# Keys of a multi-head attention: laid out by TensorE with a 0/1 matrix, or by a trip through DRAM

## Chip, cores, metric

The kernel runs on one core of a Trainium2 chip. The metric is device time in microseconds (us) of one execution, given as the median of several. Beside it there is one profiled execution, whose trace gives every instruction's start and duration.

## What is computed

Four layers work on x, 2048 tokens by 128 features, in float32. In the order of the reference:

```python
x = x + 0.5 * L0_ffn(norm(x)); x = x + L0_attn(norm(x)); x = x + 0.5 * L0_ffn(norm(x))
x = x + 0.5 * L1_ffn(norm(x)); x = x + L1_attn(norm(x)); x = x + 0.5 * L1_ffn(norm(x))
x = x + 0.5 * L2_ffn(norm(x)); x = x + L2_attn(norm(x)); x = x + 0.5 * L2_ffn(norm(x))
x = x + 0.5 * L3_ffn(norm(x)); x = x + L3_attn(norm(x)); x = x + 0.5 * L3_ffn(norm(x))
```

L0 is a low-rank product and a causal attention of one head, L1 a mixture of eight experts and a convolution. The parts that matter here come after them. L2_ffn is a gated two-layer product (silu(gate) * up, then down). L2_attn and L3_attn have 16 heads of 8 features with rotary position encoding; L3_attn is causal. L3_ffn is called twice: it holds a 16-head attention of its own whose scores are scaled per query by a sigmoid, a norm, and eight experts of which each token takes one:

```python
scores = einsum('bhqd,bhkd->bhqk', q, k) / sqrt(hd)
scores = scores * (sigmoid(einsum('bhsd,hd->bhs', q, scale_w)) * 2)[..., None]
out = softmax(scores) @ v
x = ln(src + (out * sigmoid(out @ gate_w + gate_b)) @ out_w)
x = ln(x + selected_expert(x) * weight)
```

So four big attentions over 2048 tokens and 16 heads run one after the other: L2's (rope2), that of the first L3_ffn (gated0), L3's own (rope3, causal), and that of the second L3_ffn (gated1).

## The kernel before

The tokens are cut into four chunks c of 512. For each of the four attentions `attend` (L856) walks through steps. A unit is a query chunk and a group g of four heads, so there are 16 units. In every step it may issue three things on TensorE. `score` makes a 128x1024 piece of q·k into the tile `sn`, and VectorE reduces its maximum. `weight` makes the transposed piece k·q into `st`, with the maxima already subtracted by extra rows, and ScalarE takes the exponential into `pr`. `accumulate` multiplies by the values into `av`. A unit's weights can start only when its scores are complete and its maxima have been turned and written back into the query tile.

There are three modes. "fill" runs from an attention's first step until its first weight; "core" is the steady state; "drain" begins when all its scores are issued and the first scores of the next attention take their place. Outside is "free". Norms and projections for the next layer run as side tasks (`beside`): at every step the first two in the list each issue one more part. Their order on each engine is otherwise fixed when the kernel is built.

A head has 8 features. Queries and keys are split into a rounded part (hi) and the rest (lo), so that a product of 64 rows holds hi, lo and two cross terms, and two rows of ones carry the maxima. The key tile `kp` has 128 rows (two heads of 64 rows), 8 head pairs and 2048 tokens. Its rows for one head are khi, klo, khi, klo (32 rows), two rows of ones and 30 of zeros. The projection gives hi and lo in another order: features of all heads along the 128 rows. `send("k", c)` (L688) therefore writes hi and lo to DRAM (`dk`, two DMAs of 256 KB), and `load_keys` (L707) reads them back into place with eight DMAs of 128 KB per chunk, issued by SP (SyncE). Queries go the same way through `dq`, and `begin` (L865) reads those of one unit back with two DMAs. SP issues its DMAs in order. `head_buffers` (L1408) fills the rows of ones and zeros of `kp` by eight DMAs of 512 KB from a small table `rest`.

The norm is `norm` (L177): statistics on VectorE, `inv_sqrt` (L161) with a shift, a subtraction and three Newton steps of three VectorE operations on 128x4 elements. Outside the drain ScalarE then applies scale and shift (`on_act`), for which one more VectorE operation makes `nb`. `ring` (L583) hands out most temporary 128x512 tiles from ten buffers; `wide_tile` hands out the buffers of `pr`. `put` (L600) copies a small product out of PSUM. `Experts.run` gathers tokens and weights with indirect DMAs on Pool (GpSimd), multiplies, writes to DRAM, gathers back with 16 indirect DMAs (`yg`, L1350), and `tail` norms each chunk.

Of the kernel before, what the change touches and what calls it, by code (L numbers as in the profile page):

```python
# [11 lines left out]
F32 = mybir.dt.float32  # L12
F32R = mybir.dt.float32r
I32 = mybir.dt.int32
# [17 lines left out]
NG = 4  # L32
NEG = -1.0e30
# [9 lines left out]
def tile_macaron(ctx: ExitStack, tc: tile.TileContext, a: dict, out: bass.AP):  # L43
# [8 lines left out]
    turn = {"load": 0, "evac": 0, "q": 0, "qp": 0}  # L52
# [15 lines left out]
    order = {"pinned": False, "mode": "free"}  # L68
# [25 lines left out]


    ident = const.tile([P, P], F32, name="ident")
    make_identity(nc, ident)
    anti = const.tile([P, P], F32, name="anti")
# [32 lines left out]
    iota_pi = const.tile([P, P], I32, name="iota_pi")  # L131
# [17 lines left out]
    for n in ("shift", "aT", "bT", "cT"):  # L149
        kr_in.append(const.tile(list(a[n].shape), F32, name=n))  # L150
        loads[len(kr_in) % 2].dma_start(out=kr_in[-1], in_=a[n])
# [9 lines left out]
    def inv_sqrt(pool, var, shape, tag):  # L161
        v = pool.tile(shape, F32, tag=tag + "_v", name=tag + "_v")
        vec.tensor_scalar_add(v, var, 1e-5)
        g = pool.tile(shape, I32, tag=tag + "_g", name=tag + "_g")
        vec.tensor_single_scalar(g, v.bitcast(I32), 1, op=ALU.logical_shift_right)
        vec.tensor_scalar(g, g, -1.0, float(0x5F3759DF), ALU.mult, ALU.add)
        r = pool.tile(shape, F32, tag=tag + "_r", name=tag + "_r")
        prev = g.bitcast(F32)
        for _ in range(3):
            h = pool.tile(shape, F32, tag=tag + "_h", name=tag + "_h")  # L170
            vec.tensor_tensor(h, prev, prev, ALU.mult)
            vec.scalar_tensor_tensor(h, h, -0.5, v, ALU.mult, ALU.mult)
            vec.scalar_tensor_tensor(r, h, 1.5, prev, ALU.add, ALU.mult)
            prev = r
        return r

    def norm(src, dst, on_act=False):  # L177
        stats = small.tile([P, TC, 6], F32, tag="ln_stats", name="ln_stats")
        mv = small.tile([P, TC, 2], F32, tag="ln_mv", name="ln_mv")
        for t in range(TC):  # L180
            vec.bn_stats(stats[:, t, :], src[:, t, :])
            vec.bn_aggr(mv[:, t, :], stats[:, t, :])
        rstd = inv_sqrt(small, mv[:, :, 1], [P, TC], "ln")
        if on_act:
            nb = small.tile([P, TC], F32, tag="ln_nb", name="ln_nb")
            vec.scalar_tensor_tensor(nb, mv[:, :, 0], -1.0, rstd, ALU.mult, ALU.mult)
        for t in range(TC):
            if on_act:
                nc.scalar.activation(  # L189
                    dst[:, t, :], src[:, t, :], AF.Identity, bias=nb[:, t : t + 1], scale=rstd[:, t : t + 1]  # L190
                )
            else:
                vec.tensor_scalar(
                    dst[:, t, :], src[:, t, :], mv[:, t, 0:1], rstd[:, t : t + 1], ALU.subtract, ALU.mult
                )
# [387 lines left out]
    def ring(name, tag="w", shape=(P, CW), bufs=10):  # L583
        return pools["ring"].tile(list(shape), F32, tag=tag, name=name, bufs=bufs)
# [15 lines left out]
    def put(dst, src):  # L600
        if order["mode"] == "drain":
            vec.tensor_copy(dst, src)
        elif order["mode"] == "fill":
            nc.scalar.copy(dst, src)
        else:
            evac(dst, src)
# [61 lines left out]
    class Heads:  # L668
# [3 lines left out]
        def __init__(self):  # L672
            self.current = False
            self.queries = {}
            self.units = [(qc, g) for qc in range(NC) for g in range(NG)]
            self.scores, self.weights = [], []
            for u in self.units:
                nk = u[0] + 1 if self.causal else NC
                nkb = (u[0] + 1) * TC if self.causal else NT
                if u == self.units[0]:  # L680
                    self.scores += [(self, u, t, kc) for kc in range(nk) for t in range(TC)]
                else:
                    self.scores += [(self, u, t, kc) for t in range(TC) for kc in range(nk)]
                self.weights += [(u, kb) for kb in range(nkb)]
            self.scored = 0
            self.waiting_keys, self.loaded, self.sent, self.valued, self.ready = [], set(), set(), set(), set()

        def send(self, which, c):  # L688
            hi, lo = ring("hi"), ring("lo")
            yield from self.project(which, c, hi.bitcast(F32R), lo.bitcast(F32R))  # L690
            parts = (hi, lo, lo, hi) if which == "q" else (hi, lo)
            d = (dq if which == "q" else dk)[c]
            for n, part in enumerate(parts):
                queue().dma_start(out=d[:, n * HD : (n + 1) * HD, :], in_=part)
            if which == "q":
                self.sent.add(c)
            elif self.current:
                self.load_keys(c)
            elif order["mode"] == "drain":
                self.load_keys(c, (0,))  # L700
                self.waiting_keys.append((c, (1,)))
            else:
                self.waiting_keys.append((c, (0, 1)))
            yield 1


        def load_keys(self, c, halves=(0, 1)):  # L707
            for h in halves:
                ps = slice(4 * h, 4 * h + 4)
                for j in range(2):  # L710
                    for n in range(2):
                        r = j * KD + n * 2 * HD
                        nc.sync.dma_start(
                            out=kp[r : r + 2 * HD, ps, c * CW : (c + 1) * CW].bitcast(F32),
                            in_=rows_of(dk[c], j)[:, ps, :],
                        )
            if 0 in halves:
                self.loaded.add(c)

        def prepare(self, c):  # L720
            yield from self.normed(c)
            self.ready.add(c)
            yield from self.send("k", c)
            if c == 0:
                yield from self.send("q", 0)
# [14 lines left out]
        def query(self, c):  # L740
            yield from self.send("q", c)
# [114 lines left out]
    def attend(A, carried, follow, after=None):  # L856
# [3 lines left out]
        A.current = True  # L860
        for c, halves in A.waiting_keys:
            A.load_keys(c, halves)
# [139 lines left out]
        beside = [[0, task] for task in (*carried, own)]  # L1002
# [3 lines left out]
        while nw < len(weights) or last:  # L1006
# [12 lines left out]
            if s and s[3] not in B.loaded:  # L1019
                s = None  # L1020
# [28 lines left out]
            for entry in beside[:2]:  # L1049
                if entry[0] <= n:  # L1050
                    later = next(entry[1], None)
                    if later is None:
                        beside.remove(entry)
                    else:
                        entry[0] = n + later
# [11 lines left out]
        A.current = False  # L1067
# [24 lines left out]
    class Experts:  # L1092
# [82 lines left out]
        def run(self, carried, after):  # L1175
# [76 lines left out]
            def turned(b):  # L1252
# [7 lines left out]
                for k in range(n):  # L1260
                    s = s0 + k
                    xt = ring("xt", "xt", (P, D), 4)
# [134 lines left out]
    dk = [dram.tile([NH, 2 * HD, CW], F32, name=f"dk{c}") for c in range(NC)]  # L1397
    dq = [dram.tile([NH, 4 * HD + 2, CW], F32, name=f"dq{c}") for c in range(NC)]
    def zero_tables():
        with tc.tile_pool(name="zero2", bufs=1) as tmp:  # L1400
            zero = tmp.tile([KD, 2, CW], F32, name="zero2")
            nc.vector.memset(zero, 0.0)
            for c in range(NC):
                nc.sync.dma_start(out=dq[c][:, 4 * HD :, :], in_=zero[0:NH, :, :])
            nc.vector.memset(zero[0:2, 0, :], 1.0)
            nc.sync.dma_start(out=rest, in_=zero[:, 0, :])

    def head_buffers(pool):  # L1408
# [4 lines left out]
        for j in range(2):  # L1413
            r = slice(j * KD + 4 * HD, (j + 1) * KD)
            for c in range(NC):
                nc.sync.dma_start(
                    out=kp[r, :, c * CW : (c + 1) * CW].bitcast(F32),
                    in_=rest[0:n, :].unsqueeze(1).to_broadcast([n, NH // 2, CW]),
                )
            for qp in qps:  # L1420
                nc.sync.dma_start(
                    out=qp[r, :, :].bitcast(F32), in_=rest[2 : n + 2, :].unsqueeze(1).to_broadcast([n, 2, CW])
                )
        nc.gpsimd.memset(va_flat, 1.0)
        return kp, va_flat, qps

    w3p = ctx.enter_context(tc.tile_pool(name="w3p", bufs=1))
    w2p = ctx.enter_context(tc.tile_pool(name="w2p", bufs=1))
    with tc.tile_pool(name="w1p", bufs=1) as w1p:
# [17 lines left out]
    kp, va_flat, qps = head_buffers(heads)  # L1447
# [5 lines left out]
    pools["av"] = ctx.enter_context(tc.tile_pool(name="av_ps", bufs=1, space=PSUM))  # L1453

# [8 lines left out]
    experts = [Experts(w3, g) for g in gated]  # L1463
    for c in range(NC - 1):
        finish_all([l2_chunk(c, w2), rope2.prepare(c)])
    carried = [chain([l2_chunk(NC - 1, w2), rope2.prepare(NC - 1)])]
# [23 lines left out]
def _layout(i):  # L1490
# [44 lines left out]

    sw = np.zeros((NH, HD, NH, HD), f)
# [36 lines left out]
```

## Time and profile before

| | |
|---|---|
| median of 3 runs | 4061.76 us (4051.71 to 4081.86) |
| profiled execution | 4074.4 us |
| its span | 4072.6 us |
| its mean granted TensorE clock | 0.885 |
| TensorE busy | 3557.4 us (87%) |
| VectorE busy | 3141.5 us (77%) |
| ScalarE busy | 2329.1 us (57%) |
| Pool busy | 215.0 us (5%), 262 instructions |

The page puts busy times per engine first, then the span in 40 slices, the DMA queues, the chain that ended last, the costliest groups of instructions and the DMA issues. A line of the groups reads: line in the code, engine, operation, output <- inputs, shapes, count | busy time, mean of one in ns | idle time of the engine just before, and what ended it. PE is TensorE, PEld its weight loads, DVE VectorE, ACT ScalarE, POOL GpSimd, SPq the issues of SyncE's queue. A row of a stage table has the window, then busy time and count per engine, the granted clock (1.00 is full), the DMA engines' busy share and GB/s.

The trace gives the stages:

| stage | us |
|---|---|
| L0 and L1 | 0 to 664 |
| L2_ffn and rope2's keys, first scores, first weights at 851 | 664 to 851 |
| rope2 core; drain | 851 to 1466; to 1565 |
| fill of gated0, first weights at 1663 | 1565 to 1663 |
| gated0 core and drain | 1663 to 2345 |
| experts 0, rope3's keys, first score 2573.5, first weights 2594.8 | 2345 to 2595 |
| rope3 core; drain | 2595 to 3077; to 3166 |
| fill of gated1, first weights at 3211 | 3166 to 3211 |
| gated1 core and drain | 3211 to 3896 |
| experts 1, tail, store | 3896 to 4072.6 |

### The profile page before, as it was taken

To read this page: it belongs to the slowest core of one execution; us is meant where nothing else is said; L and a number is where in the kernel's file an instruction comes from. 1 tells how busy PE (TensorE), PEld (TensorE's weight loads), DVE (VectorE), ACT (ScalarE), POOL (GpSimd) and SP (SyncE) were. 2 spreads that over 40 slices of the span, in tenths; PEclk is the share of its full clock that TensorE was granted. 3 is DMA by queue.
4 is the path that set the end of the run, shared out by engine and by line. 5 is a ranking of instruction groups with operands and counts; after the bars stand their busy time and mean duration, and the time that the engine had idled before them with its cause. 6 is when DMAs were issued, how large, how long until landed. Compare 5 with 4: busy or idle time off the path is not lost. (4 is left out here: it accounts for less than half of the span.)

```text
span 4072.6 us, 72035 instructions
## 1 busy us (share of the span) xinstructions
PE 3557.4 (87%) x29080; PEld 1680.4 (41%) x29080; DVE 3141.5 (77%) x5645; ACT 2329.1 (57%) x4436; POOL 215.0 (5%) x262
## 2 busy tenths in 40 slices
PE   8789898689999995899999965599997899999965
PEld 8566664333333342333333343243333333333334
DVE  3855443579999975899999745689997799999844
ACT  1222122158888862688888722246675488888732
POOL 2000000100000000000000033100000000000013
PEclk8889798779999997899999966668998799999966
DMA  2100003220000002100000022400002200000012
GB/s 71 25 1 1 1 1 87 62 63 7 10 7 10 4 13 57 50 9 9 7 10 4 9 70 77 110 20 10 10 2 62 54 10 7 10 7 7 7 42 74
DMA packets 71532, 111.91 MB, mean 27 GB/s; under 512 B 9712, under 2 KB 29920, under 8 KB 70944
## 3 DMA queue, kind: packets, MB, share of 16 engines
q1 hardware_dynamic: 57536, 77.81, 7.2%
q0 software_dynamic: 7088, 20.81, 2.1%
q10 hardware_dynamic: 6576, 8.69, 0.8%
q8 instruction: 229, 3.75, 0.4%
q14 instruction: 103, 0.84, 0.1%
HBM read 74.47 MB, written 31.75 MB: 26 GB/s over the span
## 5 line engine op out<-in xcount | busy, mean ns | idle before, releaser
L83 DVE TENSOR_REDUCE h_mx<-sn 128x2 f32<-128x1024 f32 (+1 forms) x1856 | 2206.3, 1197 | 141.4 <-PE sn L886 119.8
L942 ACT ACTIVATE pr<-st 128x512 f32<-128x512 f32 x3712 | 1972.7, 585 | 518.7 <-PE st L75 335.7
L75 PE MATMUL av<-pr,va 128*32 128x256 f32 x14592 | 1191.4, 399 | 10.9 <-ACT h_ot L971 10.9
L75 PE MATMUL st<-qp,kp 64*128 64x512 f32 x3712 | 998.4, 500 | 49.2 <-ACT pr L942 45.6
L886 PE MATMUL sn<-kp,qp 64*128 64x512 f32 (+3 forms) x3712 | 812.1, 416 | 126.6 <-DMA qp<-dq 46.1
L75 PEld LDWEIGHTS st<-qp,kp 64*128 64x128 f32 x3712 | 394.4, 188 | 818.1 <-ACT pr L942 441.8
L75 PEld LDWEIGHTS av<-pr,va 128*32 128x32 f32 x14592 | 293.1, 109 | 664.7 <-issue 626.8
L886 PEld LDWEIGHTS sn<-kp,qp 64*128 64x128 f32 x3712 | 388.7, 195 | 186.6 <-issue 99.8
L75 PE MATMUL h<-xnT,w_l_w12T 128*128 128x512 f32 x512 | 250.1, 611 | 1.7 <-DVE xnT L65 1.7
L554 ACT ACTIVATE hid<-h 128x512 f32<-128x512 f32 x128 | 76.4, 597 | 301.4 <-PE h L75 301.4
L75 PEld LDWEIGHTS po<-w_l_w3T,hid 128*128 128x128 f32 x1024 | 131.2, 193 | 69.1 <-DVE hid L555 47.2
L563 DVE SCALAR_TENSOR_TENSOR x<-po,gate,x 128x128 f32<-128x128 f32 x256 | 71.9, 344 | 100.4 <-PE po L75 100.3
L75 PE MATMUL po<-w_l_w3T,hid 128*128 128x128 f32 x1024 | 139.9, 279 | 1.3 <-DVE hid L555 1.3
L555 DVE TENSOR_TENSOR hid<-hid,h 128x512 f32<-128x512 f32 x128 | 87.2, 683 | 55.1 <-PE h L75 55.1
L75 PEld LDWEIGHTS h<-xnT,w_l_w12T 128*128 128x128 f32 x512 | 90.2, 197 | 66.1 <-issue 62.6
L1270 POOL DMA_INDIRECT wt<-in_b_wt,w_row_i x30 | 28.8, 960 | 1436.6 <-DVE slot_i L83 1395.0
L915 ACT CAST h_mT<-mt_ps 8x512 fp32r<-8x512 f32 x64 | 36.9, 576 | 100.4 <-PE mt_ps L93 100.2
L83 DVE BATCH_NORM_STATS2 st<-ph 128x6 f32<-128x256 f32 x46 | 19.9, 432 | 87.0 <-PE ph L75 87.0
L223 POOL TENSOR_TENSOR x<-x,w_b_n2b 128x512 f32<-128x512 f32 x8 | 10.1, 1266 | 1301.1 <-DVE rows L83 1133.7
L93 PE MATMUL xn_tp<-ident,xn_t 128*128 128x128 f32 x64 | 20.1, 406 | 66.3 <-ACT xn_t L189 62.7
L83 DVE TENSOR_TENSOR sn<-sn,mask_qk 128x256 f32<-128x256 f32 x128 | 54.2, 426 | 30.7 <-PE sn L886 29.3
L83 DVE TENSOR_TENSOR st<-st,mask_kq 128x128 f32<-128x128 f32 x256 | 63.3, 291 | 14.0 <-PE st L75 13.4
(391 smaller groups left out, 2627.5 us busy)
## 6 DMA issues: line engine op xcount, KB each, us to landing
qp<-dq SPq DMA_DIRECT2D x128, 136.0 KB
kp<-dk SPq DMA_DIRECT2D x128, 128.0 KB
dq<-hi SPq DMA_DIRECT2D x23, 256.0 KB
dq<-lo SPq DMA_DIRECT2D x23, 256.0 KB
wt<-in_b_wt SPq DMA_DIRECT2D x16, 258.0 KB
kp<-rest SPq DMA_DIRECT2D x8, 512.0 KB
dk<-lo SPq DMA_DIRECT2D x16, 256.0 KB
qp<-h_mT SPq DMA_DIRECT2D x256, 4.0 KB
```

The costliest lines, as they stand in the source:

```text
L75: pin(nc.tensor.matmul(dst, lhsT=lhsT, rhs=rhs, start=start, stop=stop))
L83: ins = method(*args, **kw)
L93: pin(nc.tensor.transpose(dst, src, ident))
L223: nc.gpsimd.tensor_tensor(xs, xs, row.unsqueeze(1).to_broadcast([P, TC, D]), ALU.add)
L554: nc.scalar.activation(hid[:, hb, :], p_1, AF.Silu)
L555: nc.vector.tensor_tensor(hid[:, hb, :], hid[:, hb, :], p_2, ALU.mult)
L563: nc.vector.scalar_tensor_tensor(x[:, i, :], po[:, t, :], gate[:, i, e : e + 1], x[:, i, :], ALU.mult, ALU.add)
L886: pin(nc.tensor.matmul(sc[:, j, :wd], lhsT=qp[r, p, t * P : (t + 1) * P], rhs=kp[r, 2 * g + p, kc * CW : kc * CW + wd], start=True, stop=True,
L915: nc.scalar.copy(mT, pt)
L942: nc.scalar.activation(pr[:, off:CW], sc[:, off:], AF.Exp, scale=A.scale)
L1270: nc.gpsimd.indirect_dma_start(wts[k], None, a["b3_wt"], bass.IndirectOffsetOnAxis(ap=w_row_i[:, s - E : s - E + 1], axis=0),)
```

## The change

**Keys.** `send` is split: `send_queries` keeps the trip of the queries, and `keys` has the projection write hi and lo directly into `kp`, in the place of group 2 (`PARK`). `spread(c, g)` then makes the rows of group g by four products (64 rows by 128, 512 columns) with a matrix of zeros and ones, `spread_w`, a new input that two DMAs load. The copy out of PSUM adds a bias column that is 1 in the rows of ones, so that the constant rows of `kp` need no DMA any more. In the fill the copies are two ScalarE instructions of 128x512 out of two small banks; elsewhere one instruction of 128x1024 out of the banks of the scores, on VectorE in the drain and on ScalarE otherwise. Group 2 is spread last, over its own source. In the fill, and for chunk 0 of the causal attention, all four groups are spread at once; otherwise group 0 only, and the rest becomes a side task of the next `attend` (`rest_of_keys`), placed ahead of values and queries. Scores now wait for a chunk and a group, not for a chunk.

**Side tasks.** The first three of the list run side by side, not two.

**Norms.** `inv_sqrt` takes shift and subtraction in one operation. Where `on_act` holds, that is outside the drain and in the experts' tails, the Newton steps run on Pool, four operations each, and `nb` takes two Pool operations.

**Buffers.** While the first three chunks of L2 are prepared, `ring` hands out its own buffers and those of `pr` in turn. Gathered token rows (`xt`) come from the ring and not from four buffers of their own. `put` always uses ScalarE outside the drain. Some constants move to a pool that is freed after L1.

```diff
@@ inv_sqrt, norm @@
-        vec.tensor_single_scalar(g, v.bitcast(I32), 1, op=ALU.logical_shift_right)
-        vec.tensor_scalar(g, g, -1.0, float(0x5F3759DF), ALU.mult, ALU.add)
+        vec.tensor_scalar(g, v.bitcast(I32), -0.5, float(0x5F3759DF), ALU.mult, ALU.add)
...
+            if on_pool:
+                nc.gpsimd.tensor_tensor(h, prev, prev, ALU.mult)
+                nc.gpsimd.tensor_tensor(h, h, v, ALU.mult)
+                nc.gpsimd.tensor_scalar(h, h, -0.5, 1.5, ALU.mult, ALU.add)
+                nc.gpsimd.tensor_tensor(r, h, prev, ALU.mult)
...
-        rstd = inv_sqrt(small, mv[:, :, 1], [P, TC], "ln")
+        rstd = inv_sqrt(small, mv[:, :, 1], [P, TC], "ln", on_pool=on_act)
...
-            vec.scalar_tensor_tensor(nb, mv[:, :, 0], -1.0, rstd, ALU.mult, ALU.mult)
+            nc.gpsimd.tensor_tensor(nb, mv[:, :, 0], rstd, ALU.mult)
+            nc.gpsimd.tensor_scalar(nb, nb, -1.0, None, ALU.mult)
@@ ring, put @@
+        if tag == "w" and order["spare"]:
+            turn["ring"] += 1
+            if turn["ring"] % 2:
+                return wide_tile(name)[:, 0:CW]
...
-        elif order["mode"] == "fill":
+        else:
             nc.scalar.copy(dst, src)
-        else:
-            evac(dst, src)
@@ Heads @@
+        def keys(self, c):
+            cs = slice(c * CW, (c + 1) * CW)
+            hi, lo = (kp[:, 2 * PARK + n, cs] for n in range(2))
+            yield from self.project("k", c, hi, lo)
+            groups = [0, 1, 3, PARK]
+            now = 4 if order["mode"] == "fill" or self.causal and c == 0 else 1
+            for g in groups[:now]:
+                yield from self.spread(c, g)
+            self.waiting_keys += [(c, g) for g in groups[now:]]
...
+        def spread(self, c, g):
+            cs = slice(c * CW, (c + 1) * CW)
+            both = order["mode"] != "fill"
+            if both:
+                ps = banks("spread")
+                out = [ps[:, k, :] for k in range(2)]
             else:
-                self.waiting_keys.append((c, (0, 1)))
+                out = [bank("spread") for _ in range(2)]
+            for k in range(2):
+                p = 2 * g + k
+                r = slice(p // 4 * KD, (p // 4 + 1) * KD)
+                for n in range(2):
+                    mm(out[k], spread_w[r, p % 4, n, :], kp[r, 2 * PARK + n, cs], start=n == 0, stop=n == 1)
+            if both:
+                dst = kp[:, 2 * g : 2 * g + 2, cs]
+                if order["mode"] == "drain":
+                    vec.tensor_scalar_add(dst, ps, one_rows)
+                else:
+                    nc.scalar.activation(dst, ps, AF.Identity, bias=one_rows, scale=1.0)
+            else:
+                for k in range(2):
+                    nc.scalar.activation(kp[:, 2 * g + k, cs], out[k], AF.Identity, bias=one_rows, scale=1.0)
+            self.loaded.add((c, g))
             yield 1
...
-        def load_keys(self, c, halves=(0, 1)):
-            for h in halves:
-                ps = slice(4 * h, 4 * h + 4)
-                for j in range(2):
-                    for n in range(2):
-                        r = j * KD + n * 2 * HD
-                        nc.sync.dma_start(
-                            out=kp[r : r + 2 * HD, ps, c * CW : (c + 1) * CW].bitcast(F32),
-                            in_=rows_of(dk[c], j)[:, ps, :],
-                        )
+        def rest_of_keys(self):
+            for c, g in sorted(self.waiting_keys, key=lambda e: (e[0], (0, 1, 3, PARK).index(e[1])) if self.causal
+                               else ((0, 1, 3, PARK).index(e[1]), e[0])):
+                yield from self.spread(c, g)
@@ attend @@
-        beside = [[0, task] for task in (*carried, own)]
+        beside = [[0, task] for task in (*carried, A.rest_of_keys(), own)]
...
-            if s and s[3] not in B.loaded:
+            if s and (s[3], s[1][1]) not in B.loaded:
...
-            for entry in beside[:2]:
+            for entry in beside[:3]:
@@ Experts, head_buffers, the calls @@
-                    xt = ring("xt", "xt", (P, D), 4)
+                    xt = ring("xt")[:, 0:D]
...
-            for c in range(NC):
-                nc.sync.dma_start(
-                    out=kp[r, :, c * CW : (c + 1) * CW].bitcast(F32),
-                    in_=rest[0:n, :].unsqueeze(1).to_broadcast([n, NH // 2, CW]),
-                )
...
+    order["spare"] = True
     for c in range(NC - 1):
         finish_all([l2_chunk(c, w2), rope2.prepare(c)])
+    order["spare"] = False
```

## The prediction

> **What bounds the kernel now.** I read the page's busy shares and slices first, then the busy time by stage, then in each stage the wait that ends last on TensorE. The stages:
>
> ```profile
> core 0: us, PE busy (x) PEld busy (x) DVE busy (x) ACT busy (x) POOL busy (x), PEclk, DMA share, GB/s
> 664.00:700.00 36.00, 20.40 (x59) 10.09 (x57) 11.83 (x54) 7.72 (x17) 6.24 (x4) 0.78 0.87 185
> 750.00:851.00 101.00, 60.91 (x165) 26.93 (x164) 59.05 (x81) 8.84 (x15) 15.56 (x17) 0.63 0.32 84
> 1000.00:1100.00 100.00, 99.53 (x956) 38.22 (x952) 96.89 (x95) 85.72 (x161) 0.00 (x0) 1.00 0.02 7
> 1565.00:1663.00 98.00, 59.16 (x206) 31.27 (x208) 54.49 (x116) 17.45 (x34) 3.79 (x3) 0.72 0.20 45
> 2545.00:2595.00 50.00, 12.49 (x56) 8.28 (x56) 21.62 (x57) 3.42 (x7) 4.89 (x5) 0.56 0.43 102
> 3166.00:3211.00 45.00, 31.17 (x92) 17.34 (x92) 20.84 (x43) 9.56 (x18) 2.52 (x2) 0.59 0.27 63
> ```
>
> The row at 1000 us is an attention core: TensorE 99.5% busy at full clock, VectorE 97%. No key is made or moved there, so the change can do nothing for these some 2,300 us. The other rows are the changeovers between layers, where no engine is full and a chain runs: norm, projection, keys to DRAM and back, scores, maxima, first weights. I call them T1 (664 to 851 us), T2 (1466 to 1663), T3 (2503 to 2595) and T4 (3077 to 3211). Of the score matmuls' waits on the page,
>
> ```profile
> L886 PE MATMUL sn<-kp,qp 64*128 64x512 f32 (+3 forms) x3712 | 812.1, 416 | 126.6 <-DMA qp<-dq 46.1
> ```
>
> most of the idle 126.6 us ended when queries arrived (46.1). The score tile's own view, which counts its weight loads too, gives 48.5 us ending with queries and 31.8 with keys. That is about what a shorter way for the keys can touch.
>
> **T3, the largest piece.** The timeline of TensorE, then of SP's queue:
>
> ```profile
> 2543.66 1.68 PE L75 MATMUL v_ps<-w_l_v,xnT 128*128 128x128 f32 x10
> 2573.51 0.44 PE L886 MATMUL sn<-kp,qp 64*128 64x128 f32 x1 [28.16 <-DMA qp<-dq]
> ```
> ```profile
> 2551.80 0.53 SPq L694 DMA_DIRECT2D dk<-lo  x1
> 2552.37 15.29 SPq L713 DMA_DIRECT2D kp<-dk  x19
> 2568.21 7.74 SPq L871 DMA_DIRECT2D qp<-dq  x6
> ```
>
> The queries of chunk 0 lay in DRAM by about 2531 us, but their reading back is issued behind 19 key loads (15.29 us), which wait themselves for chunk 2's keys. All of these issues go. Then the queries could be there about 5.3 us (2568.2 to 2573.5, issue to use) after they are written, near 2541, so the stall passes to TensorE's own order: its previous work ends at 2545.3, the norms ahead come later by about 5 (below), and of the spread matmuls 36 stand ahead of the first score: chunk 0's 16 fit into earlier gaps, the other 20 at 0.43 us cost 8.6. First score at about 2559: 14 gained, not 28. Bounds: 25 if the spreads fill gaps only, 2 if they run evacuation by evacuation.
>
> **T1.** The 4 MB of constant key rows saturate the DMA engines (0.87 of 664 to 700). VectorE, which works in order, stands behind the rotation tables; then TensorE waits 9.35 us for a copy queued behind them:
>
> ```profile
> DVE rot L83 <- DMA cos<-in_l_cos: 6.7, 2, 6.0
> DVE rot L83 <- DMA sin<-in_l_sin: 6.0, 1, 6.0
> PE sn L886 <- DMA kp<-dk: 13.9, 2, 12.9
> ```
>
> The chunks' first projections start 34.5 us apart (668.5, 703.0) with this load and 25.1 (703.0, 728.1) without: −9.4. In the fill the chunk-3 keys' trip costs 13.9; a spread ready after some 4 takes its place: −10. Against these, five slower norms on the chain (+7.5), spreads (+3), and one VectorE operation less in eight norms (8 x 0.2 = −1.6). Sum −10.5, bounds −22 and +5. The second ring I put at 0: TensorE's built order stays chunk by chunk, and I found no wait there that a ring buffer ends.
>
> **T2.** Drain: TensorE stands 13.3 us (1546.4) and 2.7 us before the first gated score. Key issues lie among SP's query issues, but the queries' own DRAM trip stays: −6 (0 to −16). Fill: keys arrive 5.5 us late, replaced by a spread: −3. Three chunks instead of two are now worked side by side in the drain, which takes the rest of chunk 2 (4 gate/up and 12 down matmuls, 4 transposes, one key projection) from the fill. At cold rates that is 7 us: −7, with +2 back in the drain, where TensorE was busy 77 of 99 us. The count of scores in drain and fill doesn't move. Two norms +3, spreads +3. Sum −8.
>
> **T4.** Drain stall 13.2 us: −6 as in T2. Fill: keys 3.9 late, −1.5; one norm +1.5; spreads +3, more per us than elsewhere, as TensorE is busy for 31 of the 45 us. Sum −3.
>
> **A spread's price.** No row shows it. The nearest is the score matmul, also 64 rows by 512: its tile view gives 217 ns at least, 393 in the median and 794 at most. I take 0.22 us each at full clock and 0.43 cold. Four make a spread, plus two ScalarE copies of 0.59 (the exp of 128x512 takes 585 ns). 64 spreads are 256 matmuls, 55 to 110 us of TensorE time, nearly all in changeovers with 30 to 60% idle; hence the small shares above. If that cover is missing, see the third rival. In the causal core three spreads remain beside a TensorE some 92% busy: 12 x 0.22, +3 (0 to +8).
>
> **Newton steps on Pool.** 26 norms move (26 ln_nb operations on VectorE). Each leaves 10 dependent VectorE operations, spaced 0.20 us (2.0 us), for 14 on Pool.
>
> ```profile
> L83 DVE SCALAR_TENSOR_TENSOR ln_h<-ln_h,ln_v 128x4 f32<-128x4 f32 x192 | 31.9, 172 | 3.7
> L457 POOL COPY cz<-cT 64x1 f32<-64x1 f32 x32 | 6.0, 188 | 1.5
> L784 POOL TENSOR_TENSOR rot<-rot 128x512 f32<-128x512 f32 x16 | 20.2, 1262 | 144.2 <-DVE rot L83 126.9 <-DVE h_m L83 10.5 <-DVE ln_mv L83 5.3
> ```
>
> Pool's smallest row takes 188 ns, 0.23 with its gap. I take 0.25 for [128,4]: 3.5 us, +1.5 a norm; bounds 0.19 (+0.7) and 0.35 (+2.9). [...] I go by the small row.
>
> Pool's queue matters as well. All 16 gathers of an expert layer (0.95 + 0.30 us each) now stand ahead of its tail's Newton steps, where VectorE had done the early chunks during the gathers. At the end of the kernel:
>
> ```profile
> 4056.89 0.95 POOL L1350 DMA_INDIRECT yg<-og,slot_i  x1 [0.30 <-issue]
> ```
>
> After 4057.84 come 4 x 14 operations, 56 x 0.23 = 12.9 us when interleaved: the last at 4070.7, where VectorE's last ln_nb began at 4065.8. +5 with nothing to hide it (bounds +3 and +9). After the first experts the same queue gives the +5 used in T3: three norms, 42 operations, stand before its first transpose, against 8 us now between the last gather and that transpose.
>
> **Small parts.** Before 664 us 38 norms lose one 0.16 us operation, as do the experts' inner norms; I count −3 (0 to −8). Copies going to ScalarE in the core, and gathered rows in the common ring: 0. ScalarE is 86% busy and the ring has ten buffers; the bounds are ±3 each.
>
> **Sum.** −3 −10.5 −8 −14 −3 +3 +5 = −30.5 us. The profiled execution took 4074.4 (span 4072.6, 1.8 around it), so 4044 on that scale; it lies 12.6 above the median 4061.8, which gives 4031, 0.75% faster.
>
> **Rivals.**
> - *The clock comes back.* The four fills run at 0.56 to 0.72. [...] If spreads fill the gaps and the fills reach 0.9, their TensorE time shrinks by 60.9 x 0.30 + 59.2 x 0.20 + 12.5 x 0.38 + 31.2 x 0.34 = 45 us: 3986. Against it: many short waits remain, and VectorE's 16 reductions of 1.23 us per unit don't shrink.
> - *The wait only moves.* Queries still go through DRAM. If their trip ends every drain and T3, and chunk 3's chain every fill, only T1's 9.4 and some 10 elsewhere stay, against 15 of costs: 4057.
> - *Slower: spreads in series ahead of chunk 3's chain.* In each non-causal fill 13 spreads stand in TensorE's in-order queue between that chain's steps, with three small banks. A score pair, on the two halves of the rows, takes 0.44 to 0.50 us together; a spread's four lie on one half, so I count them singly: 1.7 us cold, with a copy after, about 2.5 each. 39 x 2.5 = 97 in place of my 9: 4120. It cancels the gain from 1.0 us of path per spread and makes 1% slower from 2.05. For it: T4's fill has 14 us of idle TensorE for 22 of spreads. Against: T1 and T2 have 39 or more idle, and ScalarE is nearly free.
>
> **How the numbers follow.** About 1% (41 us) is what a measurement can tell from no change. Forecast 0.40 (0.14 beyond 1% faster, 0.26 within); clock 0.30, faster; moved wait 0.08, within; serial spreads 0.22, slower. So 0.44, 0.34, 0.22. The likeliest case alone covers 4005 to 4055. The range goes from 3965, past the clock case, to 4090, half-way into the slow one.
>
> **What would show it.** Right: first causal score 10 to 25 us nearer to the last gather; T1 shorter by some 10; last ln_nb about 5 us later after the last gather; spread matmuls at 0.22 to 0.43 us. Wrong: Pool's 128x4 operations over 0.35 us; the fills from last accumulation to first weights longer than 98 (T2) or 45 us (T4); fills at clocks over 0.85, which is the first rival.

## The result and the profile after

The changed kernel takes 4199.2 us (median of 4, 4197.6 to 4203.8) against 4071.1 for the kernel before on the same chip: a ratio of 1.032, 95% interval 1.0275 to 1.0368. It is 3.2% slower, some 128 us, where 0.75% faster was forecast. Executions of one kernel differ, too: in the largest series the kernel before took from 4055 to 4083 us (43 executions), and its medians in the series behind the runs below lie between 4067.5 and 4069.7, so a difference of a few us between two runs means nothing.

Cutting both traces at the first and last matmuls of each stage (us of the profiled executions) shows where the time went:

| stage | before | after | change |
|---|---|---|---|
| L0 and L1 | 668.5 | 662.7 | −5.8 |
| T1: preparation, to the first rope2 score | 81.6 | 104.2 | +22.6 |
| T1: fill, to the first weights | 101.1 | 95.5 | −5.6 |
| four cores together | 2335.6 | 2332.2 | −3.4 |
| four drains together | 316.0 | 359.9 | +43.9 |
| T2: fill of gated0 ("the fill before gated0") | 97.9 | 79.6 | −18.3 |
| experts 0 and 1, to their last product | 273.1 | 343.7 | +70.6 |
| T3: last product of experts 0 to the first weights | 115.1 | 116.6 | +1.5 |
| T4: fill of gated1 | 45.6 | 55.3 | +9.7 |
| end of the kernel, after the last expert product | 38.0 | 46.4 | +8.4 |

Each column is one execution. Two stages differ between executions even where nothing was edited in them: in the kernel whose only edit is the gathered rows (below), the fill of gated0 took 103.6 us and the causal core 471.7, where the kernel before has 97.9 and 482.4. Differences of that size in these two are not read as effects.

Line numbers moved with the change: L75, L83 and L886 of before are L76, L84 and L920 here. The page's busy times and the row of the new matmuls:

```profile
PE 3659.3 (87%) x29336; PEld 1740.0 (41%) x29336; DVE 3104.3 (74%) x5322; ACT 2402.5 (57%) x4543; POOL 283.1 (7%) x615
L76 PE MATMUL spread<-kp,spread_w 64*128 64x512 f32 x256 | 105.9, 545 | 22.3 <-ACT kp L784 17.8
```

The stage table of the changed kernel, with the columns of the one shown of before (busy us per engine, granted clock, DMA share, GB/s):

```profile
core 0: us, PE busy (x) PEld busy (x) DVE busy (x) ACT busy (x) POOL busy (x), PEclk, DMA share, GB/s
659.00:700.00 41.00, 25.26 (x60) 11.35 (x60) 7.80 (x31) 10.55 (x21) 11.32 (x32) 0.70 0.22 65
1000.00:1100.00 100.00, 99.54 (x960) 38.18 (x952) 97.05 (x91) 86.02 (x161) 0.00 (x0) 1.00 0.02 7
1598.00:1677.00 79.00, 58.52 (x218) 32.32 (x216) 43.45 (x65) 30.25 (x52) 8.09 (x30) 0.78 0.05 17
3228.00:3262.00 34.00, 33.65 (x96) 23.02 (x97) 3.49 (x14) 17.82 (x30) 4.05 (x15) 0.50 0.01 3
```

The core row is the same, as forecast. The first row's DMA share fell from 0.87 to 0.22: the 4 MB of constant rows are gone, and yet that stage grew. The last row is in the fill of gated1: TensorE, 17 of 24 us busy in before's same place, has hardly a gap left (33.65 of 34 us busy), at a granted clock of 0.50.

### The profile page after: what moved, and what is told of

Its sections match the earlier page's. It is cut to its first block, busy times and chain, and to the rows that moved or that the text cites. A ratio compares the mean times of both kernels' runs of the same rounds, so it can differ in the third digit from the quotient of the medians.

```text
span 4196.3 us, 72417 instructions
## 1 busy us (share of the span) xinstructions
PE 3659.3 (87%) x29336; PEld 1740.0 (41%) x29336; DVE 3104.3 (74%) x5322; ACT 2402.5 (57%) x4543; POOL 283.1 (7%) x615
## 5 line engine op out<-in xcount | busy, mean ns | idle before, releaser
L84 DVE TENSOR_REDUCE h_mx<-sn 128x2 f32<-128x1024 f32 (+1 forms) x1856 | 2206.8, 1197 | 148.7 <-PE sn L920 122.5
L76 PE MATMUL av<-pr,va 128*32 128x256 f32 x14592 | 1189.9, 398 | 10.4 <-ACT h_ot L1005 10.3
L76 PE MATMUL st<-qp,kp 64*128 64x512 f32 x3712 | 995.5, 499 | 52.4 <-ACT pr L976 49.9
L920 PE MATMUL sn<-kp,qp 64*128 64x512 f32 (+3 forms) x3712 | 805.6, 411 | 56.9 <-DVE h_mx L84 31.4
L76 PEld LDWEIGHTS st<-qp,kp 64*128 64x128 f32 x3712 | 393.2, 187 | 818.9 <-ACT pr L976 440.0
L76 PEld LDWEIGHTS av<-pr,va 128*32 128x32 f32 x14592 | 293.9, 110 | 662.7 <-issue 625.0
L920 PEld LDWEIGHTS sn<-kp,qp 64*128 64x128 f32 x3712 | 387.2, 193 | 107.0 <-DVE h_mx L84 44.6
L76 PE MATMUL h<-xnT,w_l_w12T 128*128 128x512 f32 x512 | 250.0, 611 | 2.1 <-DVE xnT L66 2.1
L76 PEld LDWEIGHTS po<-w_l_w3T,hid 128*128 128x128 f32 x1024 | 131.9, 194 | 70.0 <-DVE hid L573 48.5
L76 PE MATMUL po<-w_l_w3T,hid 128*128 128x128 f32 x1024 | 140.4, 280 | 1.4 <-DVE hid L573 1.3
L84 DVE BATCH_NORM_STATS2 st<-ph 128x6 f32<-128x256 f32 x46 | 19.9, 432 | 151.3 <-PE ph L76 151.3
L76 PE MATMUL spread<-kp,spread_w 64*128 64x512 f32 x256 | 105.9, 545 | 22.3 <-ACT kp L784 17.8
L76 PEld LDWEIGHTS h<-xnT,w_l_w12T 128*128 128x128 f32 x512 | 90.2, 197 | 64.9 <-issue 61.7
L748 ACT ACTIVATE kp<-spread,one_rows 128x512 fp32r<-128x512 f32 x92 | 60.3, 684 | 55.4 <-PE spread L76 53.5
L76 PEld LDWEIGHTS spread<-kp,spread_w 64*128 64x128 f32 x256 | 59.6, 254 | 56.3 <-ACT kp L784 21.5
```

Source lines behind the costliest of these rows:

```text
L76: pin(nc.tensor.matmul(dst, lhsT=lhsT, rhs=rhs, start=start, stop=stop))
L84: ins = method(*args, **kw)
L748: nc.scalar.activation(kp[:, 2 * g + k, cs], out[k], AF.Identity, bias=one_rows, scale=1.0)
L920: pin(nc.tensor.matmul(sc[:, j, :wd], lhsT=qp[r, p, t * P : (t + 1) * P], rhs=kp[r, 2 * g + p, kc * CW : kc * CW + wd], start=True, stop=True,
```

## The experts: where gathered rows got their tiles

This edit alone cost more than any other, and I had put it at 0. Pool's timeline in the first experts, before and then after (`xt` are token rows, `wt` weights, gathered in Pool's order):

```profile
2404.15 0.95 POOL L1263 DMA_INDIRECT xt<-xg,who  x1 [0.30 <-issue]
2416.01 0.96 POOL L1270 DMA_INDIRECT wt<-in_b_wt,w_row_i  x1 [10.90 <-PE po L75]
```
```profile
2422.86 0.94 POOL L1296 DMA_INDIRECT xt<-xg,who  x1 [0.30 <-PE ph L76]
2446.49 0.94 POOL L1303 DMA_INDIRECT wt<-in_b_wt,w_row_i  x1 [22.68 <-PE po L76]
2452.40 0.94 POOL L1296 DMA_INDIRECT xt<-xg,who  x1 [0.30 <-issue]
```

Before, twelve row gathers (three groups) are issued ahead of the first weight gather that must wait for the previous products `po`; after, only eight. The third group's rows stand behind four weight gathers, which wait 22.7 us for tiles that TensorE still reads. The rows themselves wait for nothing. TensorE then runs out of rows again and again. Its waits for them (us in total, times, longest), before and after:

```profile
PE g_tp L93 <- DMA xt<-xg,who: 6.8, 3, 4.3
PE g_tp L94 <- DMA xt<-xg,who: 26.8, 13, 4.9
```

The first expert stage grew by 35.7 us. These waits are 20.0 of them; another 14.3 are TensorE's own busy time (92.3 to 106.6 us for the same matmuls), at a mean granted clock of 0.53 where it was 0.62.

**The one edit in the kernel before:**

```diff
-                    xt = ring("xt", "xt", (P, D), 4)
+                    xt = ring("xt")[:, 0:D]
```

> The kernel before with one edit: gathered token rows from the common ring. Theory X: both expert stages grow by about 35 us, 4135 in all, with no other stage changed. Rival: no change, 4055 to 4080.

Measured: 4139.4 us against 4069.7, 1.017 (1.0154 to 1.0189). The expert stages are 167.6 and 170.6 us, +65 together, and the wait for rows is there again:

```profile
PE g_tp L93 <- DMA xt<-xg,who: 20.4, 10, 4.9
```

**Undone in the changed kernel.** Tiles of 128x512 that serve the norms elsewhere and are idle here hold a group's four rows:

```diff
+                held = ring("xt", "xn_t", (P, TC, D), 2)
...
-                    xt = ring("xt")[:, 0:D]
+                    xt = held[:, k, :]
```

> The changed kernel, but the gathered token rows of each expert group come from a set of two tiles of their own and not from the common ring. Theory X (the common ring moves the row gathers behind the weight gathers in Pool's queue, and TensorE waits for the rows): both expert stages return from 170 and 173 us to about 135, the wait of the row transposes for gathers (26.8 us in the first stage) vanishes, and the time falls from 4199 by about 70 to 4130. Rival (the expert stages are longer because of Newton steps on Pool or of what the ring gives to the other tiles): expert stages stay at 170, time 4190 to 4205.

Measured: 4146.5 us, 53 less than the changed kernel; expert stages 140.1 and 140.1 us. The wait fell to 6.6 us, as before. Theory X holds both ways, a little below its 70 when undone: this holder is not the four tiles of before, and the stages stop at 140, not 135. That the common ring, which hands out its tiles in one sequence with all others, keeps the order builder from placing the gathers earlier is an inference; that they stand later and what this costs is shown.

## Three side tasks in the drain

TensorE's waits in the first drain of the changed kernel (reason, us in total, times, longest):

```profile
PE sn L920 <- DMA qp<-dq: 11.5, 2, 9.5
PE xn_tp L94 <- DVE xc L84: 5.4, 1, 5.4
PE xn_tp L94 <- DVE xnT L84: 5.2, 1, 5.2
PE xn_tp L94 <- DVE xn_t L84: 3.0, 1, 3.0
```

Three chunks advance in step: three norms on VectorE in a row, then three groups of transposes on TensorE, then nine gate/up pairs. Ahead of the first scores of gated0 TensorE now stands 11.5 us for queries. Before it stood 13.3, for which the profile shows no releaser, and 2.7 for queries: 4.5 less, near the 6 forecast. In this drain TensorE also has 13.8 us more to do (77.1 to 90.9 busy), mostly work that left the fill: in the kernel before with three tasks, where nothing is spread, it is 89.0. The two gated drains show the effect of order alone: no key is made there, TensorE is busy 57.8 and 58.0 us on average before and after, VectorE 43.2 both times, and yet 64 us became 74.

**Undone in the changed kernel**, in the drain alone:

```diff
-            for entry in beside[:3]:
+            for entry in beside[: 2 if order["mode"] == "drain" else 3]:
```

> The changed kernel, but in the drain only the first two side tasks run side by side (three elsewhere). Theory D (three chunks in step keep TensorE's in-order queue waiting for VectorE in the drains): the four drains (119, 74, 94, 74 us) shrink by about 40 together, the fill before gated0 grows back by some 18 and the others little, 4175. Rival (the drains are longer for the spreads and the later queries, not for the third task): drains within 3 us of what they are, and longer fills, 4195 to 4215.

Measured: 4163.3 us, 36 less. Drains 96, 61, 91 and 64 (−48 together); the fill before gated0 went back to 97 (+17).

**Alone in the kernel before** (`beside[:2]` becomes `beside[:3]` everywhere):

> The kernel before with one edit: the first three side tasks run side by side, not two. Theory D (three in step lengthen the drains by themselves): drains 99, 65, 89, 64 become about 115, 74, 92, 74 (+40), the fill before gated0 falls by 10 to 18, in all +20 to +30. Rival (three hurt only together with the spread in the drain): within 8 us of the kernel before.

Measured: 4104.7 us, 1.0085 (1.0068 to 1.0102), +35, somewhat above the expected range. Drains 125, 74, 96 and 74 (+53), fill 77.7 (−20). The longest wait in the first drain is 16.0 us for keys from DRAM, about as long as TensorE stood there before; it is not what grew. The waits for `xc` and `xnT` are there without any spread:

```profile
PE xn_tp L93 <- DVE xc L83: 5.4, 1, 5.4
PE xn_tp L93 <- DVE xnT L83: 5.4, 1, 5.4
```

So theory D holds: the drains pay more than twice what the third task takes out of the fill. How much of that is waiting for VectorE and how much work moved is separated only in the gated drains.

## Newton steps on Pool

Two successive, dependent operations of the last norm in the changed kernel:

```profile
4188.73 0.19 POOL L185 TENSOR_SCALAR ln_h<-ln_h 128x4 f32<-128x4 f32 x1
4189.01 0.20 POOL L186 TENSOR_TENSOR ln_r<-ln_h,ln_r 128x4 f32<-128x4 f32 x1
```

0.20 us each, 0.28 apart: 14 x 0.28 = 3.9 us a norm against 2.0 on VectorE. That lies between the 3.5 that I took from the small row and the 4.9 of my upper bound (14 x 0.35). From 4180 to 4188 us six single operations take 0.52 to 0.72 us, each beside a VectorE operation on two 128x512 tiles (0.66 to 0.69 us) and ending 0.05 to 0.06 us after it. One of the six:

```profile
4187.62 0.69 DVE L84 TENSOR_TENSOR x<-x,rows 128x512 f32<-128x512 f32 x1
4187.72 0.65 POOL L183 TENSOR_TENSOR ln_h<-ln_r 128x4 f32<-128x4 f32 x1
```

**Alone in the kernel before** (the `inv_sqrt` and `nb` part of the diff, without the merged shift):

> The kernel before with one edit: Newton steps and nb on Pool where ScalarE applies the norm. Theory N (each norm costs about 2 us more, and at the experts' tails Pool's queue holds the steps behind 16 gathers): tail of the kernel 38 to 45 us, the way from the first experts to the first causal score +6, the preparation of the first chunks +5, in all +15 to +25. Rival (VectorE relieved pays for it): within 5 us of the kernel before.

Measured: 4112.3 us, 1.0106 (1.0089 to 1.0123), +43. The end grew from 38.0 to 47.0, the way from the first experts to the first causal score from 93.8 to 104.4, the first preparation from 81.6 to 89.4, the fill before gated0 from 97.9 to 107.1 (of which some 6 also appear where no norm was moved, see the result). The places are as I expected, the size is above the range.

**In the changed kernel** the same part is read by difference. One kernel has the rows' tiles and the two tasks undone and keeps Pool and the second ring:

> The changed kernel with two parts undone: rows with tiles of their own, and two side tasks in the drain. It differs from the kernel with the keys' new way alone by Newton steps on Pool and the second ring. If parts add up, 4199 - 53 - 36 = 4110, and Newton on Pool with the ring cost 25 here against 43 in the kernel before. Rival (Newton costs 43 here too, and the other two overlap): 4125 to 4135.

Measured: 4106.5 us, where adding up gave 4110. Against the kernel with the keys alone (4085.0, next section) Pool and the second ring cost 21.5; no run separates the two.

## The keys' new way alone

Four parts undone: the two above, Newton steps on VectorE, `order["spare"]` never set. The merged shift and the ScalarE copies stay.

> The changed kernel with four parts undone: rows with tiles of their own, two side tasks in the drain, Newton steps on VectorE, one ring. What stays is the keys' way, the merged shift and the copies on ScalarE. If the keys' new way is what I forecast (about -25 without the Pool steps' cost of some 20): 4030 to 4050. Rival S (spreads stand in series ahead of the chains in the changeovers): over 4075, with the changeovers longer than before.

Measured: 4085.0 us, 1.0032 (1.0017 to 1.0047): about 15 us slower than before (7 to 19 by the interval). My forecast for the keys missed; rival S has the size and, in two of the four changeovers, the place. T1's preparation is 99.1 us (+17.5), its fill 97.0 (−4.1), the fill of gated0 91.5 (−6.4), T3 107.0 (−8.1), T4's fill 55.3 (+9.7). TensorE in T1:

```profile
693.43 0.79 PE L76 MATMUL spread<-kp,spread_w 64*128 64x512 f32 x1 [3.27 <-ACT kp L783]
694.16 2.07 PE L76 MATMUL pj<-xnT,w_l_qA 128*128 128x512 f32 x2
705.96 2.08 PE L76 MATMUL gu<-xc,l_wgT 128*128 128x512 f32 x2 [6.15 <-ACT xc L625]
```

The spread waits 3.27 us for the key's rounding on ScalarE, which itself stood 5.33 us for the sum on Pool, and the queries' projection stands behind it. VectorE rotates the queries only at 699.85, after 8.46 us in which it waits for that projection, ScalarE rounds them at 702.70, after 3.74 us in which it waits for Pool, and the copy `xc` of the next chunk stands behind that on ScalarE. The next chunk's first projection starts 39.7 us after the first's; it was 34.5 with the DMA wait. Before, VectorE made that copy:

```profile
702.96 2.07 PE L75 MATMUL gu<-xc,l_wgT 128*128 128x512 f32 x2 [9.35 <-DVE xc L65]
```

That `put` now uses ScalarE here may therefore be part of this loss. No run undoes it alone, so the 15 us belong to the keys' way and the copies together. The rotation tables wait for no DMA any more, and the gain is spent. T3 in the changed kernel:

```profile
2589.96 0.75 PE L76 MATMUL spread<-kp,spread_w 64*128 64x512 f32 x2 [3.55 <-ACT kp L784]
2591.32 6.62 PE L76 MATMUL spread<-kp,spread_w 64*128 64x512 f32 x14 [0.60 <-POOL kp L823]
2598.14 1.91 PE L76 MATMUL pj<-xnT,w_l_qA 128*128 128x512 f32 x2
```

16 matmuls at about half a microsecond stand ahead of the first queries: these start 18.8 us after the chunk's transposes (2579.35), and 6.0 before (2511.05, 2517.03).

**Queries first.** The first chunk's queries are projected and sent before its keys are spread:

```diff
@@ keys @@
             yield from self.project("k", c, hi, lo)
+            if c == 0:
+                yield from self.send_queries(0)
             groups = [0, 1, 3, PARK]
...
@@ prepare @@
             yield from self.keys(c)
-            if c == 0:
-                yield from self.send_queries(0)
```

> The kernel with the keys' new way alone (four other parts undone), and the first chunk's queries projected and sent before the keys of that chunk are spread. Theory Q (spreads in TensorE's in-order queue hold the first queries back, 11.5 us in the causal layer and 6 or more in the first): the way from the first experts to the first causal score falls from 82 to 70 to 74, the preparation of the first layer from 99 to 88 to 93, 4065 to 4070 in all against 4085. Rival (the queries are not what is late there; the spreads that follow are): within 5 us of 4085.

Measured: 4063.4 us, 0.9989 (0.9973 to 1.0004): 22 us less than without, and no longer different from the kernel before. T1's preparation is 92.3, as expected (−6.8); the way to the first causal score 79.2, 3 less where 8 to 12 were expected. The queries' products there begin 6 us after the transposes again:

```profile
2518.37 1.91 PE L76 MATMUL pj<-xnT,w_l_qA 128*128 128x512 f32 x2
```

In T1, chunk 2 now starts 60.1 us after chunk 0, as before (59.6), and yet the first score comes 10.7 later than before. Between the two TensorE has 15 spread matmuls that the kernel before doesn't have; that they make these 10.7 is argued, not tested.

**The late groups last.** Spreads of the other groups after values and queries (and two tasks everywhere):

```diff
-        beside = [[0, task] for task in (*carried, A.rest_of_keys(), own)]
+        beside = [[0, task] for task in (*carried, own, A.rest_of_keys())]
```

> As the run with queries first, and the other groups' spreads come after values and queries in the list of side tasks, two tasks side by side everywhere. Theory S (nine spreads of four cold matmuls, 0.5 us each, stand in each fill, 18 us of TensorE time): they move behind the first weights, where the clock is full (0.22 us each, 8 us); the fill before gated1 falls from 55 to about 43, and the first layer's and gated0's by 5 to 10; 4040 to 4060. Rival (scores wait for the late groups in the core): fills shorter, but cores longer by the same or more, 4070 to 4100.

Measured: 4110.5 us, 1.010 (1.0075 to 1.0131), +47 on the run before it. Two fills did fall, T1's to 85.9 and T4's to 41.3 (T2's did not: 91.5 to 92.7), but each core grew, by 24, 18, 14 and 19 us. The rival was right: the cores hide nothing. Which of them made it, the spreads themselves or the scores held back for their groups, this run doesn't separate.

**Two groups in the drain:**

```diff
-            now = 4 if order["mode"] == "fill" or self.causal and c == 0 else 1
+            now = 4 if order["mode"] == "fill" or self.causal and c == 0 else 2 if order["mode"] == "drain" else 1
```

> The kernel with the keys' new way alone and queries first, and in the drain groups 0 and 1 of a chunk are spread at once, not group 0 alone. Theory S (each spread of four cold matmuls costs about 2 us of a fill that is full on TensorE): the fills before gated0 and gated1 lose two to three spreads each, 4 to 6 us, the drains grow by 1 to 3: 4055 to 4060 against 4063. Rival (the drain's in-order queue pays the same or more): drains +5 or more, 4063 to 4075.

Measured: 4065.9 us, 0.9986 (0.9977 to 0.9995), in the rival's range: the fills lost 3.5 and 2.4 us, two drains grew by 5 and 9.5. No version here is faster than the kernel before by more than 0.14%.

## The waits that I had read off the kernel before

**Key loads out of SP's queue.** Keys still go through DRAM, but Pool's queue issues their loads (`nc.sync` to `nc.gpsimd` in `load_keys`).

> The kernel before with one edit: the key loads are issued by Pool's queue, not by SP's; keys still go through DRAM. Theory Q (in the causal layer the first queries wait 28 us behind key loads in SP's queue, and not for their own trip): the way from the first experts to the first causal score falls from 94 to 70 to 78, the drains by 2 to 6 each, 4040 to 4055. Rival (the queries' own trip or Pool's in-order queue takes the wait's place): 4062 to 4080.

Measured: 4071.8 us, 1.0008 (0.9996 to 1.002), no change. And yet the stall is gone, as theory Q says. SP's queue and TensorE in T3:

```profile
2544.12 8.54 SPq L871 DMA_DIRECT2D qp<-dq  x5
```
```profile
2550.41 0.30 PE L886 MATMUL sn<-kp,qp 64*128 64x128 f32 x1 [3.62 <-DMA qp<-dq]
```

The first causal score comes 28.9 us sooner after the experts (64.9 against 93.8). But the causal fill is 10.5 longer and the causal core 8.9: from the experts' last product to the core's end, 597.6 became 588.0. Even these 10 can't be put down to the edit: in the kernel with only the rows' edit, which keeps the stall, the same way took 584.9. Most of what was waited for here is waited for later, and a stall of 28 us on TensorE was worth nothing in the whole that 22 executions could show.

**Constant rows by Pool.** The eight DMAs of 512 KB become four memsets.

> As the run with key loads on Pool's queue, and the constant rows of the keys are set by Pool, not by eight DMAs of 512 KB. Theory T (these DMAs hold up the rotation tables by about 9 us before the first score): the preparation of the first layer falls from 82 to about 73, another 8 to 10 us less than the run with key loads on Pool. Rival (Pool's writes, some 14 us for each half, stand before its own rotation steps and take the same time): within 3 us of that run.

Measured: 4115.6 us, 1.012 (1.0098 to 1.0141) against the kernel before, 44 more than the run with key loads on Pool's queue. T1's preparation is 121.6 us. Pool's groups show why this was no test of the DMAs:

```profile
L1415 POOL MEMSET kp<- 32x16384 f32 x2 | 27.5, 13744 | 420.7 <-PE po L75 420.6
L1416 POOL MEMSET kp<- 2x16384 f32 x2 | 27.5, 13744 | 0.1
```

55 us in front of Pool's rotation steps. Both theories fall short, since the two-row memset costs as much as the 32-row one (13.7 us each); what the DMAs alone cost stays open.

## Why the prediction was wrong

It failed in three terms of its sum: the rows in the ring and the third side task, which I had costed near nothing, and the keys' way, whose spreads I had taken to fit into gaps. The parts of the sum against what the runs give, in us:

| part | forecast | measured | from |
|---|---|---|---|
| rows from the common ring | 0 | +53 | 4199.2 to 4146.5 |
| third side task | −5 | +36 | 4199.2 to 4163.3 |
| Newton on Pool (and second ring, 0) | +22 | +21.5 | 4106.5 to 4085.0 |
| keys' way, merged shift, copies | −47.5 | +15 | 4085.0 to 4069.7 before |
| sum | −30.5 | +125 | whole: +128 |

The forecast column takes my stage sums apart: Newton terms 7.5 + 5 + 3 + 1.5 + 5, the third task's −7 + 2, the rest the keys. The keys' way is missed by most, 62.5; the rows by 53, the third task by 41. That the parts add up was tested once, by the kernel with the first two undone (4106.5 where adding gave 4110); the last two rows are differences and would add up in any case.

- *Rows in the ring, "0".* A step that failed: I gave ±3 because the ring has ten buffers, and did not ask where the gathers would then stand in Pool's queue. Pool's order in the built kernel would have shown it, and the timeline of before showed weight gathers waiting 10.9 us for `po` in that queue.
- *The third task, "−7, with +2 back in the drain".* The second step that failed. The fill did lose time (18 to 20 us); the drains' price was mis-sized by far, 48 to 53, and I had not costed the two gated drains, which have side tasks too (+9 each).
- *T1, "−9.4" and "−10".* The third step that failed, with T3 and T4: spreads were costed as if they filled gaps. The DMA waits went. What took their place was the spread in TensorE's in-order queue, ahead of the queries: 6.8 of the 17.5 us in the preparation, and 22 of the whole, by the run with queries first. For the other 10.7 the cause stays open.
- *T3, "14 gained, not 28".* The first causal score came 3.4 us sooner (93.8 to 90.4) and the first weights 1.5 later. I had seen that TensorE's order would end the wait, but counted chunk 0's 16 matmuls as lying in earlier gaps. They pushed the first queries back by 13, though only 3 of that came back with queries first. By the runs' first scores, the keys' way alone gained 11.6 (93.8 to 82.2); the Newton steps took 5.2 of it back, as forecast, and the rows in the ring 3.0. And the stall I started from was worth nothing in the whole kernel when it was taken away by itself.
- *T4, "spreads +3".* The fill grew by 9.7 where its terms (−1.5, +1.5, +3) sum to +3, and became longer than the 45 us that I had named as a sign. The third rival named the place and mechanism, with T4's 14 us of idle time as its argument. Its price per spread was near (four matmuls in 2.0 us), its reach was not: the fills of T1 and T2 became shorter.
- *Newton, "+22".* Right in sum (21.5, second ring included) and roughly in place: between the profiled executions of the two kernels the difference is 3.5 in T1 (7.5 forecast), 3.2 in the fill of gated0 (3), 6.2 in T3 (5) and 6.7 at the end (5). The end of the changed kernel grew by 8.4, inside the bounds. The kernel before paid 43 for it; a price found in one kernel does not carry over to another.
- *The clock rival* did not occur: none of the fills came near 0.9. That filled gaps bring a fill's clock to 0.9, on which its 45 us rest, is shown by no run; with TensorE busy 33.65 of 34 us in T4's fill, it stood at 0.50. T4's whole fill went from 0.59 to 0.61, its first 34 us from 0.60 to 0.50. T2's rose from 0.72 to 0.78, but is shorter for lack of chunk 2: with two tasks in the drain it is 97 us again. One reading against this rival was off: a unit of the non-causal layers has 32 reductions, not 16.

The forecast gave "slower" 0.22 and for one mechanism alone; it was three, and the two that cost most were edits that I had put near nothing.

## What to carry to other kernels

An edit of where a tile comes from is an edit of order: look at which instructions it moves past in each in-order queue, and what those wait for, before costing it at nothing. A stall seen in the trace is an upper bound; take it away alone and see what the next stage does with it. New work put "into idle gaps" of an engine that works in order belongs behind everything that the next chain needs, queries before keys here.

## What was not expected of the hardware

TensorE stayed at half clock while the profile shows it almost never idle (it models where a matmul ends). In the fill of gated1 it is busy 33.65 of 34 us with a granted clock of 0.50 from 3228 to 3262 us, and the kernel with the keys alone shows the same (33.12 of 34 us, 0.50); in the core, as busy (99.54 of 100 us), it is 1.00. The starts of the matmuls agree with the record of the clock: a spread takes 2.0 us in this stretch and 1.0 just after it, where the clock is 0.94.

```profile
3237.83 2.07 PE L76 MATMUL spread<-kp,spread_w 64*128 64x512 f32 x4
3265.46 1.09 PE L76 MATMUL spread<-kp,spread_w 64*128 64x512 f32 x4
```

Weight loads are busy for 23.02 of these 34 us. No run here says what the granted clock goes by. I had priced a spread's matmul at 0.22 to 0.43 us; in this stretch each took 0.5.
